# Where block 1 of a gated cross-attention kernel takes its queries from: normalized tokens or transposed tokens with centred weights

## The chip, the core and the metric

The kernel runs on one core of one Trainium2 chip. The metric is the device time of one execution in microseconds (us); the median of three runs is given. The engines are named as in the profile: PE is TensorE, PEld its weight load, DVE is VectorE, ACT is ScalarE, POOL is GpSimd, SP is the queue that issues nearly all DMAs here. Each engine works through its own instructions in order; one that waits holds up those behind it.

## The reference, cut to what matters

x is (2, 2048, 512), a context per batch element is (77, 512); everything is float32.

```python
x = x + tanh(g_xattn[0]) * xattn(layernorm(x), ctx, ctx, Wq, bq, Wk, bk, Wv, bv, Wo, bo)
x = x + tanh(g_ffn[0])   * ffn(layernorm(x), w1, b1, w2, b2)

def layernorm(x):  return (x - mean(x)) / sqrt(var(x) + 1e-5)     # over the last axis
def xattn(query, key, value, ...):                                 # 16 heads of 32
    q, k, v = query @ Wq.T + bq, key @ Wk.T + bk, value @ Wv.T + bv
    return softmax(q @ k.T / sqrt(32)) @ v   @ Wo.T + bo           # per head, heads joined before Wo
def ffn(x, ...):                                                   # per-tensor 8-bit rounding, hidden 2048
    h = gelu(qlinear(x, w1, b1)); return qlinear(h, w2, b2)
```

## The kernel before

The 4096 tokens are eight blocks of 512 (`NB` = 8, `TB` = 512); blocks 0 to 3 attend to context 0, blocks 4 to 7 to context 1. All attention comes first, then the first and the second matrix of the feed-forward part over all blocks.

**A block of attention** is eight steps `s` (`k` = 8 i + s counts them over all blocks). A step is one group of four heads and half of the block's tokens. In order of the code a step holds: `shares` of step k + 1 (DVE sums `sm` and reciprocals `rs`, then POOL multiplies the exponentials `e` by them), products of the neighbouring blocks that are listed in the tables, `apply_v` for a finished group (PE `pc`, ACT `cT`), `scores` of step k + 2 (PE `ps`, DVE `mx`), `transpose_a` of this step (PE `pta` from `e`, ACT `aT`), `exponential` of step k + 2 (ACT), then sums and statistics on POOL and DVE, and last the products `behind`. In this part the order on PE, DVE, ACT, POOL and SP is that of the code (`manual_schedule`, line 693).

**Queries.** There are two ways to make them.
- Blocks 0 and 1: `norm_stats` gives mean and reciprocal sigma (`rstd`) of each token on DVE and POOL, `normalize` writes normalized tokens `xn` (DVE, line 335), `transpose_x` turns them on PE (`ptx`, line 344) and copies them out on ACT (`xnT`, line 345), and `project_q` multiplies them by `wq_sb` (`pq`, line 353).
- Blocks 2 to 7: `load_xT` loads the block's tokens already transposed from DRAM (`xT`). The mean is taken out of the weights instead: `sum_wq` (POOL), `sum_columns` (PE `pm`, ACT `wq_mean`) and `center_wq` (POOL, line 328) subtract from each column of `wq_sb` its mean. `rstd` goes along the free axis, so `write_row` writes 512 values to DRAM (line 293), `read_row` reads them back to all partitions (`rrow`, line 299), and `scale_x` multiplies `xT` by them (POOL, line 306). These blocks use a seven-product scheme (`unit_q`, with the sums `sums_wq` of the weights and `sums_x` of the tokens).

The tables `begin` (block 0), `second` (block 1), `plan` and `end` say where products stand: `p2` is `project_q` of this block's group 2, `P0` that of the next block's group 0, `q0` to `q6` and `o0` to `o6` the units of the seven-product scheme for queries and output.

**Keys and values** of context 0 are made before the steps, those of context 1 in block 0: `project_k` (PE `pk`) and `place_k` (DVE and ACT in turn, into `kb`) for group s - 3 in steps 3 to 6, `project_v` (PE `pvv`, DVE `vb`) in step 6.

**Loads.** SP issues all loads at the start: x of block 0, the weights `wk_sb`, `wq_sb`, `wv_sb`, context 1, x of block 1, `wo_sb`, the gates and biases, x of block 2, and the four quarters of w1 (`load_w`, line 641). `wk_sb`, `wv_sb`, the x of the blocks and the quarters of w1 and w2 are tiles of one pool of eight (`xblk`, line 71):

```python
xpool = ctx.enter_context(tc.tile_pool(name="xpool", bufs=NB))
def big(name):
    return xpool.tile([P, KC, TB], F32, tag="xblk", name=name)
wk_sb, wv_sb = big("wk_sb"), big("wv_sb")
```

The fourth quarter of w1 is the ninth tile of it and takes the slot of `wk_sb`. The tiles `xnT` and `xT` share two slots (`tag="xnT"`), `rrow` has one. After the start, `load_xT(i + 2)`, `write_row(i + 2)` and `read_row(i + 2)` are issued on SP in block i, the read two steps after the write.

Of the kernel before, what the change touches and what calls it, by code (L numbers as in the profile page):

```python
# [8 lines left out]
F32 = mybir.dt.float32  # L9
# [6 lines left out]
P = 128  # L16
D = 512
KC = D // P
# [24 lines left out]
def tile_flamingo_gated_block(  # L43
# [35 lines left out]
    def load_x(i, pieces=1, engines=(nc.sync,)):  # L79
        X[i] = big(f"x{i}")  # L80
        src = x[i * TB : (i + 1) * TB, :].rearrange("(t p) d -> p t d", p=P)
        n = NT // pieces
        for t in range(0, NT, n):
            engine = engines[t // n % len(engines)]
            engine.dma_start(X[i][:, t : t + n, :], src[:, t : t + n, :])

    def kchunks(w):
        return w.rearrange("(kc p) n -> p kc n", p=P)
# [44 lines left out]
        load_group(nc.sync, wq_sb, wqT, g)  # L133
    for b in range(1, B):
        load_ctx(nc.sync, b)
    load_x(1)
    xT_sb = {}

    def load_xT(i):
        xT_sb[i] = work.tile([P, KC, TB], F32, tag="xnT", name=f"xT{i}", bufs=2)  # L140
        nc.sync.dma_start(xT_sb[i], kchunks(xT[:, i * TB : (i + 1) * TB]))

    nc.sync.dma_start(wo_sb, kchunks(woT))
    nc.sync.dma_start(tg[:, 0:1], g_xattn.to_broadcast([P, 1]))
    nc.sync.dma_start(tg[:, 1:2], g_ffn.to_broadcast([P, 1]))
# [72 lines left out]
    with actx:  # L218
# [97 lines left out]
        def sum_columns(total):  # L316

            pm = bank("pm")
            nc.tensor.matmul(pm, ones, total, start=True, stop=True)
            mean = work.tile([P, D], F32, tag="rrow", name="wq_mean", bufs=1)  # L320
            nc.scalar.activation(mean, pm, AF.Copy, scale=1.0 / D)
            return mean

# [6 lines left out]
        xn = {}  # L330

        def normalize(i, t):
            mv, rstd = ln[i]
            xn[i, t] = work.tile([P, D], F32, tag="xn", name=f"xn{i}_{t}")
            nc.vector.tensor_scalar(
                xn[i, t], X[i][:, t, :], mv[:, t, 0:1], rstd[:, t : t + 1], ALU.subtract, ALU.mult
            )
# [12 lines left out]
        def project_q(i, g):  # L350
            pq = bank(f"pq{i}_{g}")
            for kc in range(KC):
                nc.tensor.matmul(  # L353
                    pq,
                    wq_sb[:, kc, g * P : (g + 1) * P],
                    (xnT if i < 2 else xT_sb)[i][:, kc, :],
                    start=(kc == 0),
                    stop=(kc == KC - 1),
                )
            if g % 2 == 0:  # L360
                qT[i, g // 2] = work.tile([P, 2, TB], F32, tag="qT", name=f"qT{i}_{g}", bufs=2)
            q = qT[i, g // 2][:, g % 2, :]
            nc.scalar.activation(q, pq, AF.Identity, bias=bq_sb[:, g : g + 1])
# [21 lines left out]
        def sums_wq(n):  # L385

            a11, a12, a21, a22 = (quarter(wq_sb, c, r) for r in range(2) for c in range(2))
            s1, s2, s3, s4 = (wq_s[:, j] for j in range(4))
            combine(
                *(  # L390
                    (s1, a21, a22, ALU.add),
                    (s2, s1, a11, ALU.subtract),
                    (s3, a11, a21, ALU.subtract),
                    (s4, a12, s2, ALU.subtract),
                )[n]
            )
# [327 lines left out]
            6: ("q2", "q3 q4 q5"),  # L724
            7: ("q6", ""),
        }
        begin = {1: ("", "p2"), 3: ("", "p3"), 5: ("", "P0"), 6: ("", "P1"), 7: ("", "P2")}
        end = {
            0: ("o0", "o1"),
            1: ("", "o2"),  # L730
# [51 lines left out]
        for i in range(NB):  # L782
            more = i + 1 < NB
            units = (begin, second)[i] if i < 2 else plan if more else end
            d = 2 if i == 1 else 1
            for s in range(2 * NG):
                g, odd = divmod(s, 2)
                k = i * 2 * NG + s
                ahead = divmod(k + 2, 2 * NG)
                front, behind = units.get(s, ("", ""))  # L790
                for task, *args in later:
                    task(*args)
                later = []

                if k + 1 < NB * 2 * NG:
                    shares(*divmod(k + 1, 2 * NG))
                products(i, front, last=False)
                if not odd and k > 0:
                    apply_v(*((i, g - 1) if s > 0 else (i - 1, NG - 1)))
                if ahead[0] < NB:  # L800
                    scores(*ahead)
                for u in range(2):
                    transpose_a(i, s, u)
                if ahead[0] < NB:
                    exponential(*ahead)

                if i == 0:
                    if s == 1:
                        total = sum_wq()
                    if s == 2:  # L810


                        nc.scalar.activation(tg, tg, AF.Tanh)
                        nc.gpsimd.tensor_scalar(bo_sb, bo_sb, tg[:, 0:1], None, ALU.mult)
                    if s in (5, 6):
                        for n in range(2):
                            sums_wq(2 * (s - 5) + n)
                    if s == 7:
                        for n in range(2):
                            sums_wo(n)  # L820
                if i == 1 and s in (1, 2):
                    sums_wo(s + 1)
                if i > 0 and s < 2:
                    for n in ((1, 2), (4,))[s]:
                        sums_c(i - 1, n)
                if more and i > 0:
                    chunks = {0: (0, 1), 1: (2, 3)} if i == 1 else {0: (0,), 1: (1, 2, 3)}
                    for kc in chunks.get(s - d, ()):
                        scale_x(i + 1, kc)
                    for n in {2: (3, 1), 3: (2,), 4: (4,)}.get(s - d, ()):  # L830
                        sums_x(i + 1, n)
                for t in range(NT):
                    if s == ((4, 5, 6, 7) if i == 0 else (4, 4, 5, 6))[t]:
                        add_bias(i, t)
                if more and s == 7:
                    sums_c(i, 3)

                if i == 0 and s in (2, 3):
                    normalize(1, 2 * s - 4)
                    normalize(1, 2 * s - 3)  # L840
                if i == 0 and s in (0, 1):
                    norm_stats(1, 2 * s)
                    norm_stats(1, 2 * s + 1)
                if i + 2 < NB:
                    steps = (5, 5, 6, 6) if i == 0 else (4, 5, 5, 6) if i + 3 == NB else (3, 4, 5, 5)
                    for t in range(NT):
                        if s == steps[t]:
                            norm_stats(i + 2, t)
                if i > 0:

                    for t in range(NT):
                        if s == ((4, 4, 6, 6) if more else (5, 5, 6, 6))[t]:
                            norm2_stats(i - 1, t, n=2 * (t % 2))
                    these = {5: (0,), 6: (1,), 7: (2,)} if more else {6: (0, 1), 7: (2, 3)}
                    for n in these.get(s, ()):
                        extreme(i - 1, n)
                if i > 1:
                    for n in {0: (3, 4), 2: (5, 6), 3: (7,)}.get(s, ()):
                        extreme(i - 2, n)
                if not more and s == 5:  # L860

                    xs0 = work.tile([P, NT, D], F32, tag="xnT", name="xs0", bufs=2)
                    for t in range(NT):
                        normalize2(xs0[:, t, :], 0, t)
                products(i, behind, last=True)
                if i == 0 and s == 2:
                    mean = sum_columns(total)
                if i == 0 and s == 3:
                    center_wq(mean)
                if i == 0 and s in (3, 4):  # L870
                    transpose_x(1, 2 * s - 6)
                    transpose_x(1, 2 * s - 5)
                if i == 0 and 3 <= s < 7:
                    for b in range(1, B):
                        place_k(b, s - 3, project_k(b, s - 3))
                        if s == 6:
                            project_v(b)
                for task, args in tasks.get(k, ()):
                    task(*args)
                if i + 2 < NB:  # L880
                    if i > 0 and s == int(i + 3 == NB):
                        load_x(i + 2)
                    if s == 4:
                        load_xT(i + 2)
                    if s == (6 if i == 0 or i + 3 == NB else 5):
                        write_row(i + 2)
                        at(k + 2, read_row, i + 2)
# [271 lines left out]
```

## Time and profile before

| | |
|---|---|
| median of 3 runs | 634.13 us (634.09 to 636.54) |
| profiled execution | 637.02 us, span of its instructions 634.8 us |
| granted TensorE clock, mean | 0.986 |
| PE busy | 599.1 us, 94% of the span |
| DVE, ACT, POOL busy | 477.6, 410.9, 330.6 us |
| steps of blocks 0 and 1 | about 31 to 130 us |

The profile is one execution, recorded by the hardware. Its times count from the first instruction. A group or a timeline row names the engine, the line of the kernel, the operation, the tiles written and read, and in brackets how long the engine was idle before it and what ended that. A busy PE is not a PE at its peak, since the ends of matmuls are modelled. The span lies 2.2 us inside the execution's own time.

### The profile page before, as it was taken

What the parts mean: (1) busy time and instruction counts of PE and PEld (TensorE: products, weight loads), DVE (VectorE), ACT (ScalarE), POOL (GpSimd) and SP (SyncE); (2) the same over time, 40 slices, a digit from 0 to 9 for tenths busy, and PEclk for the clock granted to TensorE, in tenths of its full rate; (3) what the DMA queues carried; (4) which work ended last, traced back from release to release, by engine and by line L of the source; (5) the groups of instructions that cost most, each with busy time, mean ns of one, the idle gap of its engine ahead of it and who ended that gap; (6) DMA issues with size and microseconds to landing.
All of it is one profiled execution on the core that took longest, in us unless ns stands there. A gap on an engine that the chain in (4) does not pass through costs nothing.

```text
span 634.8 us, 9361 instructions
## 1 busy us (share of the span) xinstructions
PE 599.1 (94%) x3269; PEld 372.1 (59%) x3290; DVE 477.6 (75%) x743; ACT 410.9 (65%) x922; POOL 330.6 (52%) x291
## 2 busy tenths in 40 slices
PE   3999999899999999999999969799999979999997
PEld 3556467677777777787787745344444424444444
DVE  4376658678998788777757686999999789877452
ACT  1377556777667868766676641698989979554520
POOL 3066687679787789697785361000000009998000
PEclk9999999999999999999999969899999989999999
DMA  9910340031360163240000030299999019799942
GB/s 290 359 62 1 134 148 2 1 150 67 133 216 1 19 208 118 80 144 1 17 1 1 3 149 1 83 323 324 326 352 273 9 35 366 285 366 324 377 151 84
DMA packets 51270, 94.95 MB, mean 150 GB/s; under 512 B 22219, under 2 KB 26571, under 8 KB 45464
## 3 DMA queue, kind: packets, MB, share of 16 engines
q1 hardware_dynamic: 50120, 93.67, 42.9%
q10 hardware_dynamic: 1104, 0.69, 0.4%
q8 instruction: 26, 0.43, 0.3%
q14 instruction: 20, 0.16, 0.1%
HBM read 57.11 MB, written 33.57 MB: 143 GB/s over the span
## 4 chain that ended last, share of the span: by engine, by line
PE 77%; DVE 11%; POOL 4%; ACT 4%; issue 2%; DMA 1%; ACTq 0%; POOLq 0%; DVEq 0%
PE ph L1002 17%; PE pf L1069 17%; PE pta L572 7%; PE oa L443 6%; PE ps L523 5%; PE qa L443 5%; PE ob L443 5%; PE pc L581 4%; PE qb L443 4%; PE pq L353 3%; ACT e L543 2%; POOL e L561 1%; DVE sm L557 1%; PE po L598 1%; PE pvv L261 1%
## 5 line engine op out<-in xcount | busy, mean ns | idle before, releaser
L561 POOL TENSOR_TENSOR e<-e,rs 128x616 f32<-128x616 f32 x64 | 77.9, 1217 | 97.0 <-DVE rs L559 86.5
L543 ACT ACTIVATE e<-ps,mx 128x77 f32<-128x77 f32 x512 | 117.0, 344 | 12.8 <-DVE mx L532 9.6
L1069 PE MATMUL pf<-w2q,hq 128*128 128x512 bf16 (+1 forms) x518 | 111.8, 376 | 3.1 <-DVE hq L212 2.3
L1002 PE MATMUL ph<-xqT,w1q 128*128 128x512 bf16 x501 | 111.6, 382 | 2.6 <-DVE xqT L212 1.8
L1010 ACT ACTIVATE G<-ph,b1s,s 128x512 f32<-128x512 f32 x128 | 99.3, 778 | 13.6 <-PE ph L1002 2.9
L573 ACT COPY aT<-pta 77x512 f32<-77x512 f32 x128 | 68.8, 587 | 55.2 <-PE pta L572 55.1
L1069 PEld LDWEIGHTS <-hq 128*128 128x128 bf16 x528 | 51.8, 98 | 63.0 <-DVE hq L212 3.0
L1002 PEld LDWEIGHTS <-w1q 128*128 128x128 bf16 x512 | 50.5, 99 | 63.5 <-issue 4.2
L1020 DVE TENSOR_REDUCE hmax<-G 128x1 f32<-128x1024 f32 (+1 forms) x65 | 76.7, 1196 | 6.6 <-ACT G L1010 6.6
L572 PE MATMUL pta<-ident,e 128*77 128x128 f32 x512 | 72.4, 284 | 7.0 <-POOL e L561 4.0
L557 DVE TENSOR_REDUCE sm<-e 128x8 f32<-128x616 f32 x64 | 50.4, 788 | 24.1 <-ACT e L543 24.0
L572 PEld LDWEIGHTS pta<-ident,e 128*77 128x77 f32 x512 | 56.6, 149 | 19.2 <-issue 8.0
L532 DVE TENSOR_REDUCE mx<-ps 128x8 f32<-128x616 f32 x64 | 50.2, 786 | 22.4 <-PE ps L523 22.2
L1060 POOL TENSOR_SCALAR b_sb<-b_sb,s 128x512 f32<-128x512 f32 x1 | 3.5, 3486 | 122.0 <-issue 122.0
L1062 ACT ACTIVATE Gb<-Gb,inv_h 128x2048 f32<-128x2048 f32 x22 | 43.6, 1999 | 34.2 <-DMA Gb<-h 27.9
L523 PEld LDWEIGHTS ps<-kb,qT 64*128 64x128 f32 x512 | 36.0, 186 | 37.7 <-issue 31.0
L1083 POOL TENSOR_TENSOR x<-x,b_sb 128x512 f32<-128x512 f32 x32 | 57.2, 1826 | 0.1
L523 PE MATMUL ps<-kb,qT 64*128 64x154 f32 x512 | 50.6, 317 | 0.7 <-DVE qT L489 0.5
L1091 DVE SCALAR_TENSOR_TENSOR x<-pf,s,x 128x512 f32<-128x512 f32 (+1 forms) x33 | 23.8, 730 | 30.3 <-PE pf L1069 24.3
L624 DVE TENSOR_REDUCE xm<-x 128x1 f32<-128x512 f32 x64 | 40.8, 669 | 0.0
L1063 DVE TENSOR_SCALAR hq<-Gb 128x2048 bf16<-128x2048 f32 x22 | 36.6, 1697 | 5.6 <-ACT Gb L1062 5.6
L348 POOL TENSOR_TENSOR x<-x,bo_sb 128x512 f32<-128x512 f32 x32 | 40.4, 1272 | 0.0
(140 smaller groups left out, 940.5 us busy)
## 6 DMA issues: line engine op xcount, KB each, us to landing
h<-G SPq DMA_DIRECT2D x22, 1024.0 KB, 4.9
Gb<-h SPq DMA_DIRECT2D x22, 1024.0 KB, 8.6
out_y<-x SPq DMA_DIRECT2D x31, 256.0 KB, 4.0
x<-in_x SPq DMA_DIRECT2D x7, 1024.0 KB, 6.7
xT<-in_xT SPq DMA_DIRECT2D x6, 1024.0 KB, 8.9
raw_w<-in_w2T SPq DMA_DIRECT2D x6, 1024.0 KB, 6.5
raw_w<-in_w1T SPq DMA_DIRECT2D x4, 1024.0 KB, 12.8
w_dram<-xqT SPq DMA_DIRECT2D x4, 512.0 KB, 3.2
```

The lines of the kernel that those rows point to most:

```text
L443: nc.tensor.matmul(ps[:, m * H : (m + 1) * H], a[:, c, m * P : (m + 1) * P], b[:, c, :], start=(m + c == 0 and not more), stop=(m + c == 2 ...
L523: nc.tensor.matmul(ps[:, q, u * RK : (u + 1) * RK], qT[i, g // 2][r, g % 2, t * P : (t + 1) * P], kblk[i // NBB][r, g, :], start=True, sto ...
L543: last = nc.scalar.activation(es[i, s][:, u, j * NK : (j + 1) * NK], sc[:, q, u, r, :], AF.Exp, bias=mx[:, q, u, r : r + 1], scale=-1.0,)
L557: nc.vector.tensor_reduce(sm, e4, AX.X, ALU.add)
L561: return nc.gpsimd.tensor_tensor(e4, e4, rs[:, :, :, None].to_broadcast([P, 2, HG, NK]), ALU.mult).ins
L572: nc.tensor.transpose(pt[:NK, j, :], es[i, s][:, u, j, :], ident)
L573: nc.scalar.copy(aT[i, g][:, :, t * P : (t + 1) * P], pt[:NK, :, :])
L1002: nc.tensor.matmul(ph[u], w1q[:, kc, fc * P : (fc + 1) * P], cur[:, kc, :], start=(kc == 0), stop=(kc == KC - 1),)
L1010: nc.scalar.activation(G[:, 2 * v + u, :], ph[u], AF.Gelu, bias=b1s[:, fc : fc + 1], scale=s1,)
L1020: nc.vector.tensor_reduce(hmax[:, k + u : k + u + 1], G[:, 2 * v + u : 2 * v + u + n, :], AX.XY, ALU.max, apply_absolute_value=True,)
L1069: nc.tensor.matmul(po[t, c.start][:, : c.stop - c.start], hq[:, fc, t * P : (t + 1) * P], w2q[:, fc, c], start=(fc == 0), stop=(fc == FC - 1),
L1083: nc.gpsimd.tensor_tensor(y, y, b2_sb, ALU.add)
```

## The change

Block 1 gets its queries in the second way, from `xT` and centred weights, with the plain `project_q`; block 0 stays. `load_xT(1)` is issued at the start behind x of block 1. `normalize(1, t)` and `transpose_x(1, t)` go. Group 3 of block 0's queries moves to step 2, and behind it stand the column sums and `center_wq`. `write_row(1)` is issued in step 1 and `read_row(1)` in step 2; `scale_x(1, kc)` stands in step 3. `wq_mean` uses a buffer of `xn`, no longer `rrow`. `project_k` and `place_k` of context 1 stand in steps 3 (groups 0 to 2) and 4 (group 3), `project_v` in step 4. The four `sums_wq` stand in steps 5 and 6 of block 0 and 3 and 4 of block 1, block 0's bias adds in steps 5 and 6.

```diff
--- before.py
+++ after.py
@@ -133,13 +133,14 @@
         load_group(nc.sync, wq_sb, wqT, g)
     for b in range(1, B):
         load_ctx(nc.sync, b)
-    load_x(1)
     xT_sb = {}
 
     def load_xT(i):
         xT_sb[i] = work.tile([P, KC, TB], F32, tag="xnT", name=f"xT{i}", bufs=2)
         nc.sync.dma_start(xT_sb[i], kchunks(xT[:, i * TB : (i + 1) * TB]))
 
+    load_x(1)
+    load_xT(1)
     nc.sync.dma_start(wo_sb, kchunks(woT))
     nc.sync.dma_start(tg[:, 0:1], g_xattn.to_broadcast([P, 1]))
     nc.sync.dma_start(tg[:, 1:2], g_ffn.to_broadcast([P, 1]))
@@ -317,7 +318,7 @@
 
             pm = bank("pm")
             nc.tensor.matmul(pm, ones, total, start=True, stop=True)
-            mean = work.tile([P, D], F32, tag="rrow", name="wq_mean", bufs=1)
+            mean = work.tile([P, D], F32, tag="xn", name="wq_mean")
             nc.scalar.activation(mean, pm, AF.Copy, scale=1.0 / D)
             return mean
 
@@ -353,7 +354,7 @@
                 nc.tensor.matmul(
                     pq,
                     wq_sb[:, kc, g * P : (g + 1) * P],
-                    (xnT if i < 2 else xT_sb)[i][:, kc, :],
+                    (xT_sb if i else xnT)[i][:, kc, :],
                     start=(kc == 0),
                     stop=(kc == KC - 1),
                 )
@@ -724,7 +725,7 @@
             6: ("q2", "q3 q4 q5"),
             7: ("q6", ""),
         }
-        begin = {1: ("", "p2"), 3: ("", "p3"), 5: ("", "P0"), 6: ("", "P1"), 7: ("", "P2")}
+        begin = {1: ("", "p2"), 2: ("", "p3"), 5: ("", "P0"), 6: ("", "P1"), 7: ("", "P2")}
         end = {
             0: ("o0", "o1"),
             1: ("", "o2"),
@@ -812,14 +813,18 @@
 
                         nc.scalar.activation(tg, tg, AF.Tanh)
                         nc.gpsimd.tensor_scalar(bo_sb, bo_sb, tg[:, 0:1], None, ALU.mult)
+                    if s == 3:
+                        for kc in range(KC):
+                            scale_x(1, kc)
                     if s in (5, 6):
-                        for n in range(2):
-                            sums_wq(2 * (s - 5) + n)
+                        sums_wq(s - 5)
                     if s == 7:
                         for n in range(2):
                             sums_wo(n)
                 if i == 1 and s in (1, 2):
                     sums_wo(s + 1)
+                if i == 1 and s in (3, 4):
+                    sums_wq(s - 1)
                 if i > 0 and s < 2:
                     for n in ((1, 2), (4,))[s]:
                         sums_c(i - 1, n)
@@ -830,14 +835,11 @@
                     for n in {2: (3, 1), 3: (2,), 4: (4,)}.get(s - d, ()):
                         sums_x(i + 1, n)
                 for t in range(NT):
-                    if s == ((4, 5, 6, 7) if i == 0 else (4, 4, 5, 6))[t]:
+                    if s == ((5, 5, 6, 6) if i == 0 else (4, 4, 5, 6))[t]:
                         add_bias(i, t)
                 if more and s == 7:
                     sums_c(i, 3)
 
-                if i == 0 and s in (2, 3):
-                    normalize(1, 2 * s - 4)
-                    normalize(1, 2 * s - 3)
                 if i == 0 and s in (0, 1):
                     norm_stats(1, 2 * s)
                     norm_stats(1, 2 * s + 1)
@@ -864,19 +866,18 @@
                         normalize2(xs0[:, t, :], 0, t)
                 products(i, behind, last=True)
                 if i == 0 and s == 2:
-                    mean = sum_columns(total)
-                if i == 0 and s == 3:
-                    center_wq(mean)
+                    center_wq(sum_columns(total))
                 if i == 0 and s in (3, 4):
-                    transpose_x(1, 2 * s - 6)
-                    transpose_x(1, 2 * s - 5)
-                if i == 0 and 3 <= s < 7:
                     for b in range(1, B):
-                        place_k(b, s - 3, project_k(b, s - 3))
-                        if s == 6:
+                        for n in ((0, 1, 2), (3,))[s - 3]:
+                            place_k(b, n, project_k(b, n))
+                        if s == 4:
                             project_v(b)
                 for task, args in tasks.get(k, ()):
                     task(*args)
+                if k == 1:
+                    write_row(1)
+                    at(k + 1, read_row, 1)
                 if i + 2 < NB:
                     if i > 0 and s == int(i + 3 == NB):
                         load_x(i + 2)
```

## The prediction

> **What bounds the kernel now.** I read the page first: PE's busy share and the chain that ended last.
>
> ```profile
> PE 599.1 (94%) x3269; PEld 372.1 (59%) x3290; DVE 477.6 (75%) x743; ACT 410.9 (65%) x922; POOL 330.6 (52%) x291
> ...
> PE 77%; DVE 11%; POOL 4%; ACT 4%; issue 2%; DMA 1%; ACTq 0%; POOLq 0%; DVEq 0%
> ```
>
> PE carries the kernel: a microsecond taken from PE in the attention blocks, or an idle one put into it, reaches the end. PE is busy 228.5 of the 230 us from 130 to 360, so nothing there gives a delay back. The change lies between 42 and 115 us. I read the timeline of its start, all engines, the rows that matter:
>
> ```profile
> 42.40 1.12 PE L319 MATMUL pm<-wq_total,ones 128*128 128x512 f32 x2 [0.24 <-POOL wq_total L313]
> 42.63 1.05 POOL L175 TENSOR_TENSOR rstd<-ve_a,mhalf 128x4 f32<-128x4 f32 x1
> ...
> 48.24 5.33 POOL L328 TENSOR_TENSOR wq_sb<-wq_sb,wq_mean 128x512 f32<-128x512 f32 x4
> ...
> 58.11 1.07 PE L572 MATMUL pta<-ident,e 128*77 128x128 f32 x8 [0.20 <-ACT xnT L345]
> ```
>
> Start, duration, engine; in brackets PE's idle time and its releaser. Block 1's rstd is ready at 43.7, and PE hardly waits. The last row, step 5's transposes of block 0's attention, is my reference point. Then the longest of the DMA queue's own waits (us in total, times, longest), and that queue's timeline:
>
> ```profile
> SPq L641 <- PE pk L236: 46.5, 1, 46.5
> ```
>
> ```profile
> 18.43 53.28 SPq L641 DMA_DIRECT2D raw_w<-in_w1T  x4
> 71.81 0.45 SPq L141 DMA_DIRECT2D xT<-in_xT  x1
> 74.03 0.37 SPq L293 DMA_DIRECT2D row<-rstd  x1
> 85.17 0.34 SPq L299 DMA_DIRECT2D rrow<-row  x1
> ...
> 117.52 0.37 SPq L293 DMA_DIRECT2D row<-rstd  x1
> 125.69 0.34 SPq L299 DMA_DIRECT2D rrow<-row  x1
> ...
> 249.88 0.42 SPq L641 DMA_DIRECT2D raw_w<-in_w2T  x1
> 250.69 0.55 SPq L293 DMA_DIRECT2D row<-rstd  x1
> 263.04 0.34 SPq L299 DMA_DIRECT2D rrow<-row  x1
> ```
>
> This is the view that decides. SP issues in order. The fourth load of w1 needs the slot of `wk_sb`, so it waits 46.5 us for the last product that reads `wk_sb`, `pk` of context 1, group 3; that product ends at 71.3, and everything behind it on SP leaves after it. And a row takes long to go through DRAM: from its write's issue to its read's issue 8.2 us at 117.52 with an empty queue, 11.1 us at 74.03 with 2 MB loads just ahead, 12.3 us at 250.69 with a load 0.8 us ahead.
>
> **What the change removes.** On PE four groups of `ptx` at 0.43 us (two of them lie between 49.29 and the next product at 50.16) = 1.7 us, on the path. On DVE four `xn` (2.26 + 2.51 = 4.8 us), on ACT four `xnT` copies (2.2 us): neither ends last, so nothing for them. Keys and values of context 1 are the same work in another place; block 0's bias adds move on POOL from steps 4 to 7 into 5 and 6, behind `e`, where nobody waits for them; the mean of wq takes a free `xn` buffer, which leaves `rrow` to block 1. These I cost at nothing.
>
> **What it adds on SP.** `xT` of block 1 (1 MB) is issued after x of block 1, before wo. What now lands later is wo, tg, bo, b1, x of block 2 and w1; the first needed are tg and bo, at 44.4, issued at 16 to 17 and landed by 25.5. I cost it at nothing: 19 us of cover, where one such load takes 6.5 to 9 us. Then `write_row(1)` and `read_row(1)`. In the built program they stand on SP behind all four w1 loads, because the w1 loads were issued before the loop. So the row, ready at 43.7, stays behind the load that waits for `pk` of group 3.
>
> **Who waits for that.** On POOL four `scale_x` wait for `rrow`; behind them, in order, `e` of step 5, for which PE's transposes of step 5 wait, then all the rest of PE. In front of those PE still has only `pk` group 3, `pvv` and one `scores`. There is no circle: `pk` group 3 stands before the blocked transposes. But PE must reach it first, and then wait out two DMAs and five POOL instructions. Block 2 is not late in turn: its row has rstd 22 us before its scaling (74.0 to 95.9), now without loads in front (8.2 + 4.4).
>
> **The sum**, on the clock of before. PE runs `pq` group 3 in place of the wait at 42.1 (3.44), `pm` (1.05), `ps` (0.72), `pta` (1.03), two `pk` (0.86 each): 50.1. The third `pk` needs the bank of the first, whose readers alternate between DVE and ACT (0.3 each) behind ACT's copies (1.07) and exponentials (1.84): about 51.8, so 52.7. Then `pc` (1.0), `ps` (0.72), and `pta` of step 4, its second half after ACT's `cT`: 55.2. POOL centres wq first now, from 47.3 (mean after `qT`, 0.69 + 0.63) to 52.6, and `e` of step 4 ends at 53.9, 0.5 us before PE wants it: hidden, and a microsecond per microsecond if that is gone. `pk` group 3 ends at 56.05; give it 1 us either way.
> - w1's load issues, the row write 0.5 us later as xT did (71.31 to 71.81): 56.55.
> - Row to read: 8.2 to 12.3 by the rows. A 1 MB load leaves just ahead, as at 250.69 but with less in front, so I take 11.0: 67.55.
> - The read lands 3.6 to 6.1 us after issue (the six reads of this kernel). The one followed at once by a 1 MB load, as xT of block 2 will follow here, took 5.5: 73.05.
> - Four `scale_x`: 2.49 + 2.50 by block 2's rows, 5.0, then `e` 1.22 and a hand-over: PE's step 5 transposes start at 79.4, where PE was ready at 56.05 + 3.43 + 0.72 = 60.2. A wait of 19 us.
> - Before, that point came at 58.11, with 5.15 us of `pk` (2 x 0.86) and `pvv` (3.43) still to do, and 0.5 us of small PE waits up to the block's end that I expect gone. 79.4 - 58.1 - 5.15 - 0.5 = **15.7 us later**.
>
> The clock. PE waits four times between 367 and 375.5, and then the stretches show this:
>
> ```profile
> 375.00:377.00 2.00, 1.53 (x7) 1.53 (x8) 1.97 (x5) 0.36 (x1) 1.92 (x4) 0.50 0.00 0
> 377.00:379.00 2.00, 2.00 (x6) 0.96 (x5) 2.00 (x4) 0.81 (x2) 0.63 (x1) 0.50 0.00 0
> 379.00:381.00 2.00, 2.00 (x4) 0.96 (x3) 1.32 (x3) 0.00 (x0) 0.00 (x0) 0.50 0.00 0
> 381.00:383.00 2.00, 2.00 (x11) 0.27 (x10) 0.00 (x0) 0.00 (x0) 0.00 (x0) 0.94 0.00 0
> ```
>
> (stretch, length, busy PE, PEld, DVE, ACT, POOL, then granted clock.) Waits of at most 2.3 us brought it to 0.50, and it stayed there 5.6 us from PE's resumption at 375.5; after the wait that ends at 518.5 only 2.7 us. Half of that is lost: 1.4 to 2.8, I take **2.0**; the new wait is far longer than any of those.
>
> POOL later. Two of the sums of wq move into block 1, steps 3 and 4. In step 3 POOL idles 1.9 us before `e`, so the first is free; in step 4 POOL runs without a gap from 105.3 to 115.0, where PE's `qa` already waits 1.6 us for `xt`, so the second costs **1.3** (0 if the order around it slackens).
>
> Sum 15.7 + 2.0 + 1.3 = 19.0. The profiled execution took 637.0 (span 634.8 and 2.2 around it), 2.9 over the median of the runs; I add to each: 656.0 for one profiled like it, 653.1 for the median.
>
> The rule that speaks on the longest term is in the Trainium skill, DMA: Bandwidth & Descriptors. The rows say 8.2 us or more for a row of 2 KB; its section on the anatomy of one DMA fits about 2.0 us plus bytes over 436 GB/s, for the GpSimd path, while its rules for kernel authors say that a strided last dimension falls into a descriptor for each element. By the fit, write and read would come to an estimated 4.6 us, and the kernel to about 641; the rows decide.
>
> **Rivals.**
> 1. Not slower: the row leaves SP as soon as rstd is ready, because the slot is free earlier than I read it. Row at 43.75, read issued 8.2 us later, landed 4.4 later (56.4), scaled by 61.4, `e` 62.6: PE starts step 5 at 62.7 against 63.8 (58.1 + 5.15 + 0.5), -1.1 and +1.3, 634.3. It decides if SP's write_row starts before 46. For it: rstd's time. Against it: the 46.5 us wait, and SP's order. 4%.
> 2. The same, with row and read hidden altogether (landed by 53.9): PE at 60.2, -3.6 + 1.3, 631.8. It needs row and read in 10.1 us together, where the least that the rows show is 8.2 + 3.6 = 11.8. 2%.
> 3. The wait is there but with the short ends: row 8.2, read 3.6, `pk` 1 us sooner, clock 1.4, POOL 0: 19.0 - 2.8 - 1.9 - 1 - 0.6 - 1.3 = 11.4, 645.5. Against it: the two rows with a load just ahead are 11.1 and 12.3. 8%.
>
> **How the numbers follow.** The forecast, the wait in full, has 85%; all its long ends give 19.0 + 1.3 + 0.6 + 1 + 0.8 = 22.7, 656.8. The range, 646 to 657, takes that in and most of rival 3. A change within 0.5% (3.2 us) can't be told from none by these runs: rivals 1 and 2 fall there, 6%; faster 1%, for a mechanism that I miss; slower 93%.
>
> **What would show it.** Right: SP's write_row(1) issues after w1's fourth load, near 56 to 57; its read near 67; POOL's `scale_x` of block 1 near 73, idle some 19 us before; PE idle 15 to 20 us before `pta` near 79, released by `e`; granted clock 0.50 for some microseconds after it; from block 1 on everything shifted by a constant. Wrong: write_row near 44, PE without a gap above 3 us between 50 and 80, or a row-to-read time under 6 us.

## The result, and the profile after

| | before | after |
|---|---|---|
| median, same chip | 634.86 us (6 runs, 634.09 to 636.73) | 658.81 us (6 runs, 654.26 to 661.50) |
| ratio | | 1.036 (95% interval 1.0331 to 1.0389) |
| profiled execution | 637.02 us, span 634.8 | 654.26 us, span 652.5 |
| mean granted TensorE clock, profiled | 0.986 | 0.971 |

The change makes the kernel 24 us slower. The forecast was 653.1 (646 to 657): right in direction and, in the profiled execution, in nearly every step, but the median lies 1.8 us above the range. Two questions follow: is the mechanism the forecast one, and why is the median 4.5 us above the profiled execution, when before it was below?

The page first, the lines that answer to those of before, and the clock in 40 slices of 16.3 us:

```profile
PE 598.5 (92%) x3274; PEld 369.6 (57%) x3274; DVE 473.9 (73%) x739; ACT 408.9 (63%) x918; POOL 333.8 (51%) x295
...
PEclk9999599999999999999999998899999989999999
...
PE 78%; DVE 9%; POOL 5%; DMA 3%; ACT 3%; issue 1%; ACTq 0%; POOLq 0%; SPq 0%; DVEq 0%
```

PE is busy 0.6 us less than before, in a span 17.7 us longer: it waits, and the chain's share of DMA rises from 1% to 3%, that of POOL from 4% to 5%. The one slice at 0.5 is the fifth, 65 to 82 us.

SP's own waits (us in total, times, longest), the two that matter, and then SP's timeline:

```profile
SPq L642 <- PE pk L237: 29.4, 1, 29.4
SPq L300 <- DMA row<-rstd: 25.7, 3, 10.0
```

```profile
19.72 35.41 SPq L642 DMA_DIRECT2D raw_w<-in_w1T  x4
55.23 0.45 SPq L294 DMA_DIRECT2D row<-rstd  x1
65.72 0.34 SPq L300 DMA_DIRECT2D rrow<-row  x1
66.16 0.39 SPq L140 DMA_DIRECT2D xT<-in_xT  x1
```

w1's four loads stand as one merged row until 55.13, and block 1's row leaves SP 0.1 us behind the last of them. From the row's write to its read 10.5 us pass. The timeline of the other engines at the same place:

```profile
50.02 1.12 PE L237 MATMUL pk<-ctx,wk_sb 128*128 128x77 f32 x8 [1.72 <-ACT kb L254]
...
53.72 1.01 PE L237 MATMUL pk<-ctx,wk_sb 128*128 128x77 f32 x8
...
71.53 4.92 POOL L307 TENSOR_TENSOR xT<-xT,rrow 128x512 f32<-128x512 f32 x4 [19.89 <-DMA rrow<-row]
76.41 2.39 POOL L562 TENSOR_TENSOR e<-e,rs 128x616 f32<-128x616 f32 x2
77.68 1.99 PE L573 MATMUL pta<-ident,e 128*77 128x128 f32 x8 [18.79 <-POOL e L562]
...
79.46 5.60 PE L354 MATMUL pq<-xT,wq_sb 128*128 128x512 f32 x8
```

This is the forecast chain: `pk` of group 3 at 53.72 lets the load go; POOL idles 19.89 us for `rrow`, scales, makes `e`, and PE's transposes of step 5 have waited 18.79 us for that. Then two groups run slowly: `pta` takes 1.99 us instead of 1.10, `pq` 5.60 instead of 3.60. The stretches show why (stretch, length, busy PE, PEld, DVE, ACT, POOL, granted clock):

```profile
62.00:66.00 4.00, 0.00 (x0) 0.00 (x0) 2.33 (x5) 0.00 (x0) 0.00 (x0) 0.63 0.00 0
78.00:80.00 2.00, 2.00 (x9) 1.80 (x9) 0.00 (x0) 0.88 (x2) 2.00 (x3) 0.50 0.00 0
80.00:82.00 2.00, 2.00 (x3) 0.67 (x2) 0.00 (x0) 1.98 (x9) 2.00 (x3) 0.50 0.00 0
84.00:86.00 2.00, 2.00 (x13) 0.36 (x11) 0.00 (x0) 0.69 (x1) 2.00 (x3) 1.00 0.01 4
```

The clock falls to 0.50 at 63.0, while PE idles, and comes back at 83.5, 5.8 us after PE has resumed.

I laid the two traces over each other by the first exponential of every step. The times below say how much later (+) or earlier than in the profile of before each stretch of steps makes the kernel:

| up to step 4 (the start) | steps 4 to 6 | 6 to 8 (the row, the scaling) | 8 to 15 | 15 to 17 (`qa`) | 17 to the end |
|---|---|---|---|---|---|
| -1.65 | +0.63 | +20.92 | -3.55 | +1.26 | +0.01 |

The -3.55 comes with the move of keys and values: the kernel below that moves them alone has it too. From step 4 on this is 19.3 us, where the sum said 19.0.

The start is 1.65 us shorter than in the profile of before, though PE's products there are the same and its first one even begins later (10.05 us against 9.85). The same product, `pk` of one group of context 0, first before, then after:

```profile
16.96 1.82 PE L236 MATMUL pk<-ctx,wk_sb 128*128 128x77 f32 x8
```

```profile
16.23 1.01 PE L237 MATMUL pk<-ctx,wk_sb 128*128 128x77 f32 x8
```

The clock records of the two traces begin with a rise to 1.00, at 19.42 us before and at 15.22 us after; until then the products take nearly twice their time. So the start differs by the clock, and the mean clocks, which count nothing ahead of that rise, don't show it.

### The profile page after: what moved, and what is told of

It reads as the page before. It is cut to its first block, busy times and chain, and to the rows that moved or that the text cites. A ratio compares the mean times of both kernels' runs of the same rounds, so it can differ in the third digit from the quotient of the medians.

```text
span 652.5 us, 9352 instructions
## 1 busy us (share of the span) xinstructions
PE 598.5 (92%) x3274; PEld 369.6 (57%) x3274; DVE 473.9 (73%) x739; ACT 408.9 (63%) x918; POOL 333.8 (51%) x295
## 4 chain that ended last, share of the span: by engine, by line
PE 78%; DVE 9%; POOL 5%; DMA 3%; ACT 3%; issue 1%; ACTq 0%; POOLq 0%; SPq 0%; DVEq 0%
PE pf L1070 17%; PE ph L1003 17%; PE pta L573 8%; PE oa L444 6%; PE ps L524 5%; PE qa L444 5%; PE pq L354 5%; PE ob L444 5%; PE pc L582 4%; PE qb L444 3%; ACT e L544 2%; DMA row<-rstd 2%; POOL e L562 1%; DVE sm L558 1%; PE po L599 1%
## 5 line engine op out<-in xcount | busy, mean ns | idle before, releaser
L1070 PE MATMUL pf<-w2q,hq 128*128 128x512 bf16 (+1 forms) x528 | 113.7, 379 | 2.0 <-DVE hq L213 1.8
L1070 PEld LDWEIGHTS <-hq 128*128 128x128 bf16 x528 | 52.3, 99 | 63.4 <-issue 3.5
L307 POOL TENSOR_TENSOR xT<-xT,rrow 128x512 f32<-128x512 f32 x28 | 36.8, 1336 | 19.9 <-DMA rrow<-row 19.9
```

The costliest lines, as they stand in the source:

```text
L1070: nc.tensor.matmul(po[t, c.start][:, : c.stop - c.start], hq[:, fc, t * P : (t + 1) * P], w2q[:, fc, c], start=(fc == 0), stop=(fc == FC - 1),
```

## The experiments

Where the expectations tell two theories of the median apart, A is the clock and B the row's way through DRAM. The kernel before took 635.46 us (17 runs) beside the first four kernels named here, 635.65 (17 runs) beside those without the small waits, with the fixed wait and with all moved, and 635.20 (9 runs) beside the rest.

### Is it SP's order? w1's fourth load behind the row's read

```diff
-        for j in range(4):
+        for j in range(3):
...
                 if k == 1:
                     write_row(1)
                     at(k + 1, read_row, 1)
+                    at(k + 1, load_w, "w1", 3)
```

> The changed kernel with one thing moved: the fourth load of w1 is issued behind read_row(1), no longer ahead of write_row(1). Main theory (the row waits on SP behind that load): write_row issues near 42 when rstd is ready, read near 50.5, landed near 55, scaled by 60, e of step 5 by 61.2, and PE, ready at 58.8, waits about 2.4 us instead of 18.8; the clock stays at 1.0; time 654.3 - 16.4 - 2.9 = 635.0, so 633 to 637, the same as before. Rival (the row's way through DRAM and the five POOL instructions are the cost wherever they stand, the SP order costs little): 645 or more.

Measured: 639.26 us (638.52 to 641.61, 6 runs), ratio 1.0068 (1.0052 to 1.0084). Its timeline:

```profile
42.87 0.37 SPq L294 DMA_DIRECT2D row<-rstd  x1
52.20 0.34 SPq L300 DMA_DIRECT2D rrow<-row  x1
...
57.67 4.94 POOL L307 TENSOR_TENSOR xT<-xT,rrow 128x512 f32<-128x512 f32 x4 [5.22 <-DMA rrow<-row]
...
63.84 1.10 PE L573 MATMUL pta<-ident,e 128*77 128x128 f32 x8 [0.95 <-POOL e L562]
```

One load moved gives back some 20 of the 24 us, and the wait ahead of `pta` shrinks from 18.79 to 0.95. The place of the fourth load on SP is the cause. The kernel still is 3.8 us slower than before, 2.3 us above the 637 that were expected at most. Its trace points to the clock: the clock is 0.50 for 6.83 us from 51.4, behind the 1.7 us wait of the third `pk`, and for 3.41 us from 116.2, behind a 2.90 us wait of `qa`. Both waits are in the profile of after, where the clock stayed at 1.00 behind them.

### The move of keys and values alone

The kernel before, with only `project_k`, `place_k` and `project_v` of context 1 in their new steps:

```diff
-                if i == 0 and 3 <= s < 7:
+                if i == 0 and s in (3, 4):
                     for b in range(1, B):
-                        place_k(b, s - 3, project_k(b, s - 3))
-                        if s == 6:
+                        for n in ((0, 1, 2), (3,))[s - 3]:
+                            place_k(b, n, project_k(b, n))
+                        if s == 4:
                             project_v(b)
```

> The kernel before with one part of the change alone: keys of context 1 in steps 3 (groups 0 to 2) and 4, values in step 4; block 1's queries stay with normalized and transposed tokens. Main theory: w1's fourth load issues near 56 to 62 instead of 71.3, nobody needs it then, and the time is that of before within 1.5 us (633.5 to 636.5). Rival: the third pk, which waits for the bank of the first (1.7 us in the changed kernel's profile), and the crowd of ACT and DVE work in step 3 cost PE 2 us or more, 637 and up.

Measured: 636.71 us (636.36 to 640.68, 12 runs), ratio 1.0028 (1.0014 to 1.0042): 1.3 us slower. In its trace the third `pk` waits 1.66 us for a bank, and in the next 6.83 us, from 52.3, the clock is 0.50. So this part of the change costs little; that it costs this by that wait is read from one trace and not tried by itself.

### Why the median is above the profile: first tries

The changed kernel again, unchanged:

> The changed kernel unaltered, to see what differs between its runs. Its profiled execution was 654.3 us, 1.2 from the sum, but the median 658.8. Theory A (the clock): the extra is time at half clock after PE's long wait, in windows of the same length, so the runs with a mean granted clock of 0.961 to 0.966 take 3 to 7 us more than those with 0.971, and the row's way through DRAM is the same 10 to 11 us in all. Theory B (the DMA): the row write and read take longer in the slower runs, up to 12.3 and 6.1 us instead of 10.5 and 5.8, and the clock follows from that; then this profile shows write to read over 12 us if its time is over 657.

Measured: 659.92 us (654.18 to 665.69, 6 runs), ratio 1.0368 (1.0338 to 1.0398); the profiled execution is again the fastest, 654.18. The others have a mean clock of 0.961 to 0.964 against 0.971. That fits A, but the mean alone does not say where the clock was low.

Dummy products in the long wait, to keep PE busy:

```diff
+                if k == 5:
+                    warm_pe = bank("warm_pe")
+                    turn[0] += 1
+                    for _ in range(21):
+                        nc.tensor.matmul(warm_pe, ones, wq_sb[:, 0, :], start=True, stop=True)
```

> The changed kernel with 21 products of PE (ones by a column chunk of wq, into a bank that nobody reads, 0.86 us each, 18.1 us in all) between the last product before the wait and the waiting transposes: PE is busy through the wait. Theory A (clock): the granted clock stays at 1.0 there, 2.9 us less than the profiled 654.3 = 651.4, and the median of the runs falls from 658.8 to 651 to 653 with a spread under 4 us. Theory B (the runs differ by the DMA): the median stays 3 to 5 us over the profile-like time, 655 or more, and the spread stays 7 us.

Measured: 657.44 us (654.41 to 662.65), ratio 1.0363 (1.0328 to 1.0398). A miss for this experiment: the row took 11.6 us here instead of 10.5, so the products ended 2.0 us too early, and that gap was enough:

```profile
78.89 1.22 PE L573 MATMUL pta<-ident,e 128*77 128x128 f32 x8 [2.02 <-POOL e L562]
...
79.90 5.21 PE L354 MATMUL pq<-xT,wq_sb 128*128 128x512 f32 x8
```

The clock fell for 3.41 us from 79.7. It does not tell A from B, but shows that a wait of 2.0 us does what I had put down to long ones.

The changed kernel without its two small waits of PE (group 0 of the keys one step earlier, all `sums_wq` back in block 0):

```diff
-                        sums_wq(s - 5)
+                        for n in range(2):
+                            sums_wq(2 * (s - 5) + n)
...
-                if i == 1 and s in (3, 4):
-                    sums_wq(s - 1)
...
-                if i == 0 and s in (3, 4):
+                if i == 0 and s in (2, 3, 4):
                     for b in range(1, B):
-                        for n in ((0, 1, 2), (3,))[s - 3]:
+                        for n in ((0,), (1, 2), (3,))[s - 2]:
```

> The changed kernel with its long wait kept and two small waits taken out: pk group 0 of context 1 moves into step 2, so that the third pk no longer waits 1.7 us for a bank, and all four sums of wq stand in steps 5 and 6 of block 0 again, so that qa waits 1.6 us and not 2.9. Theory A (small waits and the clock): in the profiled runs the clock stayed at 1.0 there, but in most runs it falls to 0.5 after one or both of them, for 3.4 or 6.8 us at a time, which costs 1.7 and 3.4 us and makes the median 658 to 660 where the profile says 654. Without them 654.3 - 1.3 - 1.7 = 651.3, and the median within 2 us of it, 650 to 653, spread under 4 us. Theory B (the row's DMAs take longer in most runs): the median stays 3 to 5 us over this profile's time, 654 or more, spread 6 us and more.

Measured: 655.73 us (655.23 to 658.01, 5 runs), ratio 1.0323 (1.0307 to 1.0340), the profiled execution at 655.71. Median and profile now agree and all mean clocks are 0.968 to 0.971, as A wants; but the level is above the expected one, as B wants: from the row's write to its read 12.5 us passed in this trace. `pk`'s wait has also been replaced by two of the transposes, 0.65 and 1.08 us, and the clock fell behind those, for 3.41 us.

The row replaced by work of constant length on POOL, the small waits kept:

```diff
+                        rstd_row[1] = work.tile([P, TB], F32, tag="rrow", name="rrow1", bufs=1)
+                        nc.gpsimd.memset(rstd_row[1], 1.0)
+                        for _ in range(15):
+                            nc.gpsimd.tensor_tensor(rstd_row[1], rstd_row[1], rstd_row[1], ALU.mult)
...
-                if k == 1:
-                    write_row(1)
-                    at(k + 1, read_row, 1)
```

> The changed kernel with a wait of the same length that no DMA sets: write_row and read_row of block 1 are left out, and POOL fills rrow with ones and multiplies it by itself 15 times (1.25 us each) before the scaling; block 1's tokens are so not multiplied by their reciprocal sigma. The small waits stay. Theory A (small waits and the clock): profile near 654, and the median of the runs 3 to 5 us above the fastest, as in the changed kernel, 656 to 660. Theory B (the row's DMAs): the runs lie within 2 us of each other, near 654.

Measured: 652.85 us (651.67 to 655.77, 5 runs), ratio 1.0279 (1.0259 to 1.0299), with a wait of 16.22 us ahead of `pta`. The runs still spread over 4.1 us though the wait is constant, with mean clocks of 0.969 to 0.974. Each theory seemed to hold a part.

### Both at once, and three more traces

With the constant work and without the small waits (the two edits above together):

> The changed kernel with block 1's row replaced by POOL work of constant length (block 1 thus leaves out the scaling by its reciprocal sigmas), and without the two small PE waits (one group of keys of context 1 a step earlier, all sums of wq in block 0). Theory A: with the row constant and no small waits, the mean clock of the runs differs by 0.003 or less, the spread is under 2 us (4.1 with the small waits kept), and the median is within 1 us of the profiled execution, near 650: 652.85 less the qa wait (1.3) and less some 2 us of half clock. Theory B: the row was all, so this kernel has the same spread as the one with the small waits kept, within a microsecond, and a median 1.3 lower.

Measured: 649.42 us (649.18 to 650.54, 5 runs), ratio 1.0226 (1.0212 to 1.0241), the profiled execution at 649.22. The spread falls from 4.1 to 1.4 us, the median lies on the profile. With the row constant, what was left of the spread went with the small waits, as A wants, though five runs each are few. Half clock is not gone: behind two waits of `pta` (0.65 and 1.07 us) this trace too has 3.41 us of it, but four of the five runs have the same mean clock, 0.974.

The changed kernel in three more profiled executions:

> The changed kernel, unchanged, for one more profiled execution. Open is why the median of its runs (658.8) lies 4.5 us above its profiled execution (654.26, mean clock 0.971). In every trace so far all stretches at clock 0.50 start on one grid of 3.41 us, whose position against the program differs from trace to trace (the first starts modulo 3.41: 1.57 and 1.50 in the two traces of this kernel, 0.15 in the one with the row moved early, 3.11 in the one without the small waits). Theory A: whether a PE wait of 1.7 us (third pk, near 50) or 2.9 us (qa, near 132) halves the clock hangs on where it falls on that grid; in the two traces it fell well. A trace with the grid elsewhere shows further stretches of 3.4 or 6.8 us at 0.50 behind those waits, a mean clock of 0.961 to 0.966 and 657 to 661 us, with the row's write to read at 10 to 11; one with the grid at 1.5 shows 654 to 655 and 0.971. Theory B: the time follows the row's way through DRAM; a time over 657 comes with a write to read of 13 us or more, or a read over 8, and the same stretches at 0.50.

> The same again, a fourth profiled execution of the changed kernel. Theory A: the time is 654 plus half of what its trace has at clock 0.50 above 38 us, whatever the row took within 10 to 12 us; more stretches than before stand behind the waits near 50 or 132. Theory B: time over 654 equals the row's time over 10.5 us.

> The same again, a fifth profiled execution. Theory A and theory B as in the two before it: A puts the difference from 654 into stretches at clock 0.50 behind the two small waits, B into the row's write to read.

Measured: 664.99, 659.27 and 658.22 us. The slowest of them, SP's timeline and the engines:

```profile
60.74 0.45 SPq L294 DMA_DIRECT2D row<-rstd  x1
72.89 0.34 SPq L300 DMA_DIRECT2D rrow<-row  x1
```

```profile
52.42 1.99 PE L237 MATMUL pk<-ctx,wk_sb 128*128 128x77 f32 x8 [1.71 <-ACT kb L254]
54.34 1.94 PE L582 MATMUL pc<-aT,vb 77*32 77x512 f32 x8
56.20 1.40 PE L524 MATMUL ps<-kb,qT 64*128 64x154 f32 x8
57.53 1.86 PE L573 MATMUL pta<-ident,e 128*77 128x128 f32 x8
...
79.42 4.92 POOL L307 TENSOR_TENSOR xT<-xT,rrow 128x512 f32<-128x512 f32 x4 [25.39 <-DMA rrow<-row]
85.57 1.99 PE L573 MATMUL pta<-ident,e 128*77 128x128 f32 x8 [21.17 <-POOL e L562]
```

Behind the same 1.71 us wait of `pk`, four groups run at half clock: 1.99, 1.94, 1.40 and 1.86 us against 1.12, 1.06, 0.79 and 1.10 in the first profile, 3.1 us together. All of that stands ahead of w1's fourth load, so the row leaves later too, and then needs 12.15 us instead of 10.5. Laid over the profile of before as above, all five traces of the changed kernel (us):

| execution | mean clock | up to step 4 | 4 to 6 (third `pk`) | 6 to 8 | 15 to 17 (`qa`) | from step 4 on | row's write issued to scaling begun |
|---|---|---|---|---|---|---|---|
| 654.26 | 0.971 | -1.65 | 0.63 | 20.92 | 1.26 | 19.3 | 16.3 |
| 654.18 | 0.971 | -1.75 | 0.62 | 21.13 | 1.25 | 19.3 | 16.7 |
| 658.22 | 0.969 | -0.15 | 2.10 | 21.92 | 1.26 | 21.8 | 17.2 |
| 659.27 | 0.964 | -1.50 | 3.07 | 23.49 | 1.26 | 24.2 | 18.3 |
| 664.99 | 0.961 | +0.76 | 3.62 | 22.64 | 4.45 | 27.6 | 18.7 |

(8 to 15 is -3.55 in all.) Neither theory held as it was put: 664.99 lies above A's 657 to 661, and B's row of 13 us or more never came (11.1 to 12.2). Each has a part, and a third part was in neither, the start (-1.75 to +0.76). That is the clock again: PE's first product begins at 9.2 to 10.1 us in these five traces, and the first rise of the clock comes at 15.1 and 15.2 us in the two fast ones, at 16.8, 19.2 and 21.6 us in those at 659.27, 658.22 and 664.99. Of the spread of 8.3 us from step 4 on, up to 3.0 come from the half clock behind the third `pk`, 3.2 from that behind `qa` in the one trace where it fell there, up to 2.6 from the row and the clock in its wait.

### A version with the parts that cost taken out

The row as in the first experiment; rstd ahead of wq's sums on POOL; the scaling one step later, behind `e` of step 5; group 0 of the keys one step earlier; all `sums_wq` in block 0:

```diff
-                    if s == 3:
+                    if s == 4:
                         for kc in range(KC):
                             scale_x(1, kc)
...
-                    if s == 1:
-                        total = sum_wq()
...
+                if k == 1:
+                    total = sum_wq()
...
                     at(k + 1, read_row, 1)
+                    at(k + 1, load_w, "w1", 3)
```

> The change with four things moved: the fourth load of w1 behind read_row(1); rstd of block 1 ahead of the column sums of wq on POOL; scale_x behind e of step 5; pk group 0 in step 2 and all sums of wq in block 0. Main theory: row written near 41, read issued near 50, landed near 55.5, scaled by 61 to 62, while PE still has pk, pvv, scores and the transposes of step 5 until 59.5 and then the first of four products that need one scaled chunk each: a wait of at most 2.5 us; the four ptx groups (1.7 us) are gone, so 631 to 634 against 635.5 of before. Rival (the scaling on POOL takes the place of what it removes, 5.0 us in front of e of step 6 and the sums): PE waits for e in steps 6 and 7 and at qa, and the time is 636 or more.

Measured: 634.05 us (630.79 to 636.03, 12 runs) against 635.65, ratio 0.9972 (0.9957 to 0.9986): 1.6 us faster than the kernel before on the same chip by the medians, the one version here that beats both kernels. Nothing waits for the row any more:

```profile
39.67 0.37 SPq L294 DMA_DIRECT2D row<-rstd  x1
49.27 0.34 SPq L300 DMA_DIRECT2D rrow<-row  x1
...
55.39 4.93 POOL L307 TENSOR_TENSOR xT<-xT,rrow 128x512 f32<-128x512 f32 x4
56.03 0.37 SPq L642 DMA_DIRECT2D raw_w<-in_w1T  x1
...
61.23 1.10 PE L573 MATMUL pta<-ident,e 128*77 128x128 f32 x8
```

POOL's scaling and PE's `pta` have no bracket, so neither idled. From step 4 on its trace is 1.9 us shorter than that of before. The queries of block 1 from transposed tokens are worth that little, if the row is out of the way. How much each of the moves gives was not tried by itself. The trace still has 3.41 us at clock 0.50 from 54.8 us, behind two waits of `pta` (0.91 and 0.82 us). The two fastest of the 12 runs, 630.79 and 630.91 us, have a mean clock of 0.986 where the others have 0.983 or 0.984, which fits runs without such a drop, but neither was traced.

## Why the prediction was right and where it was wrong

On the time axis of before (the profile of after with 1.65 us added for its shorter start), step by step:

- **SP's order: right.** The row's write was forecast for 56.55, and came at 56.9; the read for 67.55, at 67.4; the scaling for 73.05, at 73.2; `pta` for 79.4, at 79.3, after 18.8 us of waiting where 19 were forecast. That the fourth load causes it is shown by the kernel that moves it.
- **Rivals 1 to 3: refuted.** The row did not leave before the fourth load, and none of the short ends came.
- **15.7 us later: right to 0.6** in the profiled execution. Steps 4 to 15 are 18.0 us longer; less the half clock at `pta` and `pq` (0.89 + 2.00 = 2.9), 15.1.
- **Two sums of wq in block 1, 1.3 us: right** there, 1.26 measured; 0.04 in the trace without the small waits.
- **The sum, 19.0: right for the execution profiled** (19.3), in part by luck: its clock was 0.9 too low and its lateness 0.6 too high. For the usual execution it is too small: the middle of the five traces is 21.8.

So the mechanism was right, and the step that failed is the sizing of three terms, two in the sum and one in the step from the sum to the median:

1. **The clock, 2.0 (1.4 to 2.8).** I priced it behind the new wait alone. There it was 2.9 in the profile of after. But the prediction also had the wait for the third `pk`'s bank ("about 51.8, so 52.7") and that of `qa` (1.6 us, made longer by 1.3), and priced them as lateness only, though its own stretches from 375 showed that waits of at most 2.3 us bring the clock to 0.50. In three of five traces the first of them cost 1.5 to 3.0 us of half clock, in one the second cost 3.2.
2. **Row to read and landing, 11.0 + 5.5 = 16.5.** The five traces have 16.3 to 18.7, 17.2 in the middle; the write-to-read part is 10.5, 10.5, 11.1, 12.1 and 12.2. The bounds (12.3 and 6.1) were nearly right, the value taken was near the low end of what came.
3. **The step to the median, -2.9.** I took the distance between profile and median of before over to after. It belongs to one execution: before's has a start longer by 0.8 to 1.9 us than 10 of the 12 other traces, since its clock first rose late. After's profile was a fast one instead, 4.5 us below its median. What else made up before's 2.9 isn't shown.

The trace nearest to the median of after, at 658.22, shows both misses at about the same size: from step 4 on 21.8 us instead of 19.0, of which 1.5 is half clock behind the third `pk` and 1.0 the stretch of the row, over the first profile; and a start only 0.15 us shorter than in before's profile, so that nothing of the 2.9 taken off shows there. 2.8 + 2.9 is the distance from 653.1 to 658.8.

So the range fell short at its upper end: it took in the long ends of every term that the sum had, and the sum had no term for half clock behind the small waits; nor had the range a bound for the step to the median.

On the rule weighed in the prediction, the Trainium skill, DMA: Bandwidth & Descriptors: its fit of about 2.0 us for a small DMA, measured on the GpSimd path, would have given an estimated 641, and block 1's row took 9.3 to 12.5 us from the write's issue to the read's in all traces that have it. The rows decided rightly.

## What to carry to other kernels

A DMA issue that waits for a buffer holds every later issue of its queue: before a small, urgent transfer is put on a queue, look for what stands ahead of it, and move the load that waits. A wait of PE is priced twice, once for its length and once for the clock that it may halve. One profiled execution is one draw: where a kernel has waits near the length that drops the clock, look at several traces before its time is set against a median.

## What the runs showed of the hardware

**The clock is decided on a grid of 3.41 us.** All stretches at 0.50 within one trace start on multiples of 3.41 us from one offset, and the offset differs from execution to execution (for the five above, first stretch modulo 3.41: 1.57, 1.49, 2.14, 3.16, 1.10). I cut all 13 traces (before, after and the experiments) into those cells, from 40 us on, and summed PE's idle time in each, as the time that no product covers. Of 2160 cells at full clock, 50 have 1.74 us or more of idle time, and every one is followed by half clock; 2094 have less than 1.59 us, and none is; of the 16 between, 8 are. So about half a cell of idle time drops the clock for the next cell or more, and two short waits in one cell add up (0.65 and 1.08 us did). The 1.7 us wait of `pk` dropped it where it lay wholly or nearly so in one cell (idle 1.71, 1.59 and 1.59 in the traces at 659.27, 658.22 and 664.99), not where the grid cut it in two (1.06 and 0.66 in the profile of after); the 2.90 us wait of `qa` was cut into 1.57 and 1.33 in the profile of after, but had 2.11 us in one cell in the trace at 664.99. Where the waits lie on the grid is so a large part of why the same program has executions at 654 and 665.

**The first rise of the clock sets the length of the start.** In the 13 traces PE's first product begins at 9.1 to 10.2 us, and the clock first rises 4.8 to 12.4 us after it. Until then PE does half as much: half of this time, added to the begin of the first product, gives the differences between the starts of all 13 traces to within 0.4 us (for 664.99 against before: 0.77, measured 0.76). Why the rise comes so much later in some executions stays open.

The Trainium skill, TensorE: Matmul & The Clock Gate, Part 1, has a free-running activity window of about 3.4 us, which agrees with the grid; the rule that it names, no PE idle gaps over about 3.4 us, is too wide here, where gaps from 1.6 us on were enough.

**A row of 512 values to DRAM and back is slow and varies.** For block 1, from the write's issue to the read's, it took 10.5 to 12.5 us in the six traces with w1's fourth load just ahead of it and the long wait left empty, and 9.3 and 9.6 us in the two with nothing ahead. Why it varies by 2 us between executions of one program stays open.
